# Differential attention on one core: softmax weights of the upper 512 queries taken from the scores of their maxima, turned by 32x32 transposes and DMA

## The chip, the core and the metric

The kernel runs on one core of a Trainium2 chip. The core has five engines that each work through their own instructions in order: TensorE (PE, matmuls; PEld is its weight load), VectorE (DVE), ScalarE (ACT), GpSimd (POOL) and SyncE (SP), which here issues the DMAs. SBUF is the on-chip memory of 128 partitions, PSUM the eight banks of 128 x 512 fp32 into which matmuls write. The metric is the device time of one execution in microseconds (us).

## The reference

Four residual layers over x, two sequences of 1024 tokens of width 512: a gated linear recurrence, a feed-forward with ternary weights, a differential attention, and the same feed-forward again. The change lies in the attention:

```python
q = concat([split(x @ Wq1), split(x @ Wq2)])      # 2 x 16 heads of 32
k2, v2 = repeat(split(x @ Wk), 2), repeat(split(x @ Wv), 2)
scores = where(causal, q @ k2.T / sqrt(32), min)
p = softmax(scores)                                # 1024 x 1024 per head
y1, y2 = halves(p @ v2)
x = x + (y1 - sigmoid(x @ Wlam) * y2) @ Wo
```

Each of the two sequences has 32 query heads. All is fp32, and the scores are large enough that a softmax needs its row's maximum subtracted.

## The kernel before

The stages run one after another: recurrence, first feed-forward (`feed_forward(0, ...)`), attention, second feed-forward. The residual x lives in SBUF all the time, as 16 tiles `xres` of 128 tokens.

The attention goes through 32 pairs: `b` (sequence), `g` (group of projections), `p` and `par`. A pair holds two heads, told apart by `e` (0 or 1). `project` makes queries and keys of a group (three kinds, two halves of the sequence each: six projections for four pairs), and copies each half to the other 64 partitions by DMA (`gr<-gr`), so that a pair's heads can stand in any of four 32-row strips of the PE array: strip `2 * i + e`, where `i` picks the copy (`operands`). A matmul with 32 rows occupies one strip, and four in different strips can run together.

Every score is computed twice. `maxima_bank` (tile `s`, line 947) computes scores with queries on the partitions; DVE takes each row's maximum (lines 958 and 963; on a diagonal block with a causal mask added). `split_maxima` (POOL) splits a maximum into three bf16 parts, `turn_maxima` transposes them on PE (`mt`, line 994), so that they lie along a row. `row_phase` then computes the scores again with keys on the partitions (tile `t`, line 1024), since the product with the values needs keys there, and subtracts the maxima by a bf16 matmul of ones with `mt` (line 1034). ACT takes exp (`pr<-t`, line 1056), POOL zeroes what lies above the diagonal (line 1064) and adds two blocks of keys for the totals (line 1088). `weigh` multiplies with the values and with ones (`y`, line 1109): four 32-column strips, for two halves of the queries and two heads. The result is copied (`ys`) and sent by DMA to `share` (products) and `tot` (totals).

A pair has six steps; in each, PE does scores of this pair, maxima scores of the next, `weigh` of the step before and what `beside` holds (`at(n, step, ...)`): projections of the next group, the next sequence's normalisation, the last sequence's output. PE's order is the written one (`manual_schedule`); DVE and ACT are ordered by the planner until the end of the attention. PSUM: a ring of seven banks and one `edge` bank.

At the end of a sequence `divide` inverts the totals and folds in lambda, `combine` multiplies the factors in and subtracts the two halves, `project_out` multiplies by Wo and adds to `xres`.

## Time and profile before

The median of three runs is 2051.46 us (2048.37 to 2052.23). The profiled execution took 2050.75 us; its span, from first to last instruction, is 2049.0 us.

| stage (us from the span's start) | length | PE busy | DVE busy | ACT busy | POOL busy |
|---|---|---|---|---|---|
| recurrence 0 to 371.8 | 371.8 | 361.2 | 279.9 | 153.8 | 103.6 |
| feed-forward 371.8 to 733 | 361.2 | 361.0 | 153.5 | 144.1 | 77.8 |
| attention 733 to 1684.4 | 951.4 | 942.2 | 531.4 | 382.6 | 526.0 |
| feed-forward 1684.4 to 2049 | 364.6 | 358.0 | 136.3 | 137.7 | 77.3 |

A group's line in the profile gives line, engine, operation, output and inputs by name, shapes and count; then busy us and the mean ns of one instruction; then the idle time before them and what ended it. A timeline line gives start, length, engine and line, with idle time in brackets. A stretch's line gives for each engine its busy time and, in brackets, its instructions, then PE's granted clock (1.00 is full), the share of time that the 16 DMA engines were busy, and GB/s. An fp32 matmul stands as two records in the trace.

### The profile page before, as it was taken

Reading aid. Unit: us, or ns where it says so; the run is one execution under the profiler, and the core shown is the slowest. Engines: PE = TensorE matmul, PEld = TensorE weight load, DVE = VectorE, ACT = ScalarE, POOL = GpSimd, SP = SyncE. Lnnn points to the kernel's source line nnn. Section 1 sums busy time; section 2 is a strip of 40 time slices with the busy share of each in tenths; the row PEclk is TensorE's granted clock in tenths of the full one; section 3 lists DMA queues with packets and bytes.
Section 4 is the critical chain, followed back from the end, with each engine's and each line's share of the span. In section 5 each row is a group of like instructions: output and inputs, shape, how many; then the busy total and the mean of one; then the engine's idle time right before and its main releaser. Section 6 shows DMA issues by size and latency. Waiting matters only on the chain.

```text
span 2049.0 us, 34958 instructions
## 1 busy us (share of the span) xinstructions
PE 2022.5 (99%) x13824; PEld 1290.9 (63%) x13832; DVE 1101.0 (54%) x2375; ACT 818.2 (40%) x1453; POOL 784.6 (38%) x1131
## 2 busy tenths in 40 slices
PE   8999999999999999999999999999999999999998
PEld 4444444788888854555555545565556648888887
DVE  5876868444344434555565556455556554343422
ACT  4444343234333422444444423254444513343433
POOL 1412323122222222666666635365657732222222
PEclk9999999999999999999999999999999999999999
DMA  7121212500000111111111101202110032000000
GB/s 278 65 92 62 88 57 80 222 0 1 1 1 1 37 48 34 48 28 43 28 43 28 43 9 39 60 22 51 25 30 15 15 149 103 21 1 21 0 21 21
DMA packets 77651, 99.14 MB, mean 48 GB/s; under 512 B 41520, under 2 KB 49840, under 8 KB 77488
## 3 DMA queue, kind: packets, MB, share of 16 engines
q1 hardware_dynamic: 77488, 96.92, 14.4%
q8 instruction: 108, 1.77, 0.4%
q14 instruction: 55, 0.45, 0.1%
HBM read 58.75 MB, written 16.78 MB: 37 GB/s over the span
## 4 chain that ended last, share of the span: by engine, by line
PE 92%; DVE 5%; POOL 1%; issue 1%; ACT 1%; DMA 0%; SPq 0%; DVEq 0%; ACTq 0%; POOLq 0%
PE g L664 11%; PE u L664 11%; PE f_out L685 11%; PE y L1109 11%; PE s L947 9%; PE pq L880 8%; PE t L1024 8%; PE pv L842 3%; PE pq L328 3%; PE a_out L546 2%; PE b_out L1187 2%; PE pv L328 2%; PE pa L328 2%; PE pg L328 2%; PE pk L328 2%; PE t L1034 1%
## 5 line engine op out<-in xcount | busy, mean ns | idle before, releaser
L1056 ACT ACTIVATE pr<-t 128x512 f32<-128x512 f32 (+1 forms) x640 | 306.6, 558 | 347.5 <-PE t L1034 294.2
L679 POOL TENSOR_TENSOR ssq<-ssq,sq 128x512 f32<-128x512 f32 x120 | 154.5, 1288 | 589.6 <-ACT sq L678 589.6
L1088 POOL TENSOR_TENSOR pr<-pr,pr 128x384 f32<-128x384 f32 (+1 forms) x256 | 287.1, 1132 | 121.5 <-ACT pr L1056 114.3
L963 DVE TENSOR_REDUCE nmax<-s 128x1 f32<-128x384 f32 (+1 forms) x320 | 183.2, 581 | 201.5 <-PE s L947 200.9
L958 DVE CUSTOM_DVE_ANT_0 s<-s,causal 128x512 f32<-128x512 f32 (+3 forms) x512 | 245.6, 506 | 54.0 <-PE s L947 49.6
L947 PE MATMUL s<-gr,gr 32*128 32x384 f32 (+3 forms) x1664 | 264.0, 480 | 1.9 <-DVE nmax L963 1.9
L670 DVE TENSOR_TENSOR h<-h,u 128x512 f32<-128x512 f32 x128 | 88.1, 688 | 317.5 <-PE u L664 305.4
L664 PE MATMUL g<-xs,w 128*128 128x512 f32 x1024 | 257.7, 394 | 0.0
L685 PE MATMUL f_out<-w,hs 128*128 128x512 f32 x1024 | 254.3, 390 | 0.3 <-DVE hs L673 0.3
L664 PE MATMUL u<-xs,w 128*128 128x512 f32 x1024 | 253.2, 389 | 0.0
L1024 PE MATMUL t<-gr,gr 32*128 32x512 f32 (+3 forms) x1536 | 224.3, 528 | 1.3 <-DVE nmax L963 1.3
L664 PEld LDWEIGHTS u<-xs,w 128*128 128x128 f32 x1024 | 192.2, 188 | 40.6
L685 PEld LDWEIGHTS f_out<-w,hs 128*128 128x128 f32 x1024 | 191.5, 188 | 40.7 <-DVE hs L673 1.1
L664 PEld LDWEIGHTS g<-xs,w 128*128 128x128 f32 x1024 | 190.0, 188 | 39.6 <-issue 1.0
L947 PEld LDWEIGHTS s<-gr,gr 32*128 32x128 f32 x1664 | 172.5, 186 | 45.5 <-issue 15.3
L1109 PE MATMUL y<-pr,val 128*32 128x256 f32 (+3 forms) x3072 | 188.1, 334 | 2.5 <-POOL pr L1088 1.9
L880 PE MATMUL pq<-b_xt,w_qk 128*128 128x512 f32 x384 | 176.0, 603 | 0.8 <-DVE nmax L958 0.8
L1064 POOL TENSOR_SCALAR_AFFINE_SELECT pr<-pr 128x256 f32<-128x256 f32 x256 | 101.9, 410 | 194.5 <-ACT pr L1056 190.9
L672 ACT CAST hs<-h 128x512 fp32r<-128x512 f32 x128 | 79.4, 620 | 234.7 <-DVE h L670 234.7
L669 ACT ACTIVATE h<-g 128x512 f32<-128x512 f32 x128 | 76.6, 599 | 230.5 <-PE g L664 230.4
L1109 PEld LDWEIGHTS y<-pr,val 128*32 128x32 f32 x3072 | 80.3, 109 | 89.4 <-issue 49.7
L673 DVE TENSOR_TENSOR hs<-h,hs 128x512 fp32r<-128x512 f32 x128 | 88.6, 692 | 87.2 <-ACT hs L672 87.2
(169 smaller groups left out, 2555.0 us busy)
## 6 DMA issues: line engine op xcount, KB each, us to landing
w<-w_kept SPq DMA_DIRECT2D x32, 768.0 KB
w_kept<-w SPq DMA_DIRECT2D x16, 768.0 KB
gr<-gr SPq DMA_DIRECT2D x96, 128.0 KB
w<-in_w_gu_dram SPq DMA_DIRECT2D x32, 256.0 KB
share<-ys SPq DMA_DIRECT2D x128, 64.0 KB
x<-in_x_dram SPq DMA_DIRECT2D x16, 256.0 KB
w<-in_w_pt_dram SPq DMA_DIRECT2D x16, 256.0 KB
w_qk<-in_wq_dram SPq DMA_DIRECT2D x8, 512.0 KB
```

The costliest lines, as they stand in the source:

```text
L328: nc.tensor.matmul(po, w[:, k, ts(c, P)], xt[:, k, :], start=(k == 0), stop=(k == NKC - 1))
L664: nc.tensor.matmul(po, ws[f][:, part, ts(k, P)], xs[:, e, k, :], start=(k == 0 and e == 0), stop=(k == NKC - 1 and e == 1),)
L679: nc.gpsimd.tensor_add(ssq, ssq, sq)
L685: nc.tensor.matmul(po[j], hp[:, e, ts(j, P)], ws[f][:, 2, :], start=(f == 0 and e == 0), stop=(f == NF - 1 and e == 1),)
L880: nc.tensor.matmul(po, w[:, k, ts(kind, P)], xts[b][:, k, ts(e, BLK)], start=(k == 0), stop=(k == NKC - 1),)
L947: nc.tensor.matmul(part, queries[:, ts(j, P)], keys[:, first * P : (first + nk) * P], start=True, stop=True,)
L958: nc.vector.tensor_tensor_reduce(part, part, causal[:, BLK - part.shape[-1] :], -1.0, 3.0e38, ALU.add, ALU.min, top,)
L963: nc.vector.tensor_reduce(top, part, AX.X, ALU.max, negate=True)
L1024: nc.tensor.matmul(banks[i, e][:, at_col : at_col + nq], keys[:, ts(kb, P)], queries[:, (qb + 1) * BLK - nq : (qb + 1) * BLK], start=True, ...
L1056: nc.scalar.activation(room[i][:, e, :width], banks[i, e][:, :width], AF.Exp)
L1088: nc.gpsimd.tensor_add(both[:, e], both[:, e], second[:, e])
L1109: nc.tensor.matmul(into[rows, lo // 2 :].rearrange("p (a r) -> p a r", r=64), head, moving[:, e, :].rearrange("p (a h r) -> p a h r", h=2, ...
```

## The change

The lower four query blocks of 128 (j = 0 to 3) of each pair keep the two passes, with smaller parts: the mask is now added on PE by four small bf16 matmuls (`hide`: `select`, whose 32 rows pick 32 positions, times `hidden`), the totals are products with ones of each block of keys, and POOL adds nothing.

The upper four blocks (j = 4 to 7) have one pass. `row_scores` computes a block's scores with queries on the partitions, up to 1024 keys in a PSUM tile of two banks, one tile per head (`ps_rows`, two buffers). `row_maxima` takes the negative maximum on DVE, `row_weights` takes exp on ACT with the maximum as bias and sums the row on the way (`accum_out` into `sums`); it writes the weights in an order that puts every fourth key together. `row_turn` transposes 32x32 squares on DVE into `flat`, and four DMAs carry the squares to `full`, where keys lie on the partitions. `row_outputs`, two slots later, multiplies with the values in pieces of 64 columns. No maxima are split or turned for these blocks, and their totals come from `sums` by one transpose on PE at the end of a sequence (`turn_high`).

A pair now has four slots, one upper block in each, in the order j = 7, 5, 6, 4. The order of PE, DVE and ACT is the written one throughout. The ring of PSUM banks has three banks instead of seven. Copies of the values and of `mt` go from DVE to ACT. To make room, the residual tiles 4 to 15 are written to DRAM (`x_kept`) in the first feed-forward and read back where they are used: eight before the second sequence's normalisation (`fetched`), four for the first sequence's output, and all twelve at the end of the attention.

The core of the diff (the pools, names and the removed functions are left out):

```diff
+        def hide(i, e, part):
+            rows = ts(2 * i + e, HD)
+            for a in range(QB):
+                nc.tensor.matmul(
+                    part[:, a * HD :], select[rows, a, :], hidden[rows, a, a * HD :],
+                    start=False, stop=(a == QB - 1),
+                )
...
+        def low_scores(pair, e, i, js):
+            keys, queries = operands(pair, i, e)
+            po = ring_bank(f"s{name(pair)}_{e}_{js[0]}")
+            at_col, parts = 0, []
+            for j in js:
+                part = po[:, at_col : at_col + (j + 1) * P]
                 nc.tensor.matmul(
+                    part, queries[:, ts(j, P)], keys[:, : (j + 1) * P], start=True, stop=False
+                )
+                hide(i, e, part[:, j * P :])
...
-            nc.vector.tensor_copy(mt, po)
+            nc.scalar.copy(mt, po)
...
+        ROWS = (7, 5, 6, 4)
+        def row_scores(n, step):
+            pair, j = pairs[n], ROWS[step]
+            banks = [ps_rows.tile([P, 2 * BLK], F32, tag="rows", ...) for e in range(2)]
+            for i in range(2):
+                for e in range(2):
+                    keys, queries = operands(pair, i, e)
+                    cols = slice(i * BLK, BLK if i == 0 else (j + 1) * P)
+                    nc.tensor.matmul(
+                        banks[e][:, cols], queries[:, ts(j, P)], keys[:, cols],
+                        start=True, stop=(i == 0),
+                    )
+            for e in range(2):
+                hide(1, e, banks[e][:, j * P : (j + 1) * P])
+            return banks
...
+            nc.scalar.activation(          # row_weights
+                weights[:, :width].rearrange("p (B b k) -> p B k b", b=QB, k=HD),
+                banks[e][:, :width].rearrange("p (B k b) -> p B k b", b=QB, k=HD),
+                AF.Exp, bias=tops[:, e : e + 1],
+                accum_out=sums[b][:, j - QB, at_row : at_row + 1],
+            )
...
+            nc.vector.transpose(           # row_turn
+                flat[n][:, : 2 * width].rearrange("p (b e B q) -> p b e B q", b=QB, e=2, q=HD)[:, :, e],
+                weights[:, :width].rearrange("p (B b k) -> p b B k", b=QB, k=HD),
+            )
+            if e == 0:
+                return
+            full = spread[n, step] = row_room("full", n, step)
+            part = 2 * width // QB
+            for a in range(QB):
+                nc.sync.dma_start(
+                    out=full[:, ts(a, part)],
+                    in_=flat[n][ts(a, HD), : 2 * width].rearrange("k (b r) -> k b r", b=QB),
+                )
...
+            for B in range(j + 1):         # row_outputs
+                for half in range(2):
+                    for e in range(2):
+                        nc.tensor.matmul(
+                            y[ts(2 * half + e, HD)].rearrange("p (a q) -> p a q", q=HD),
+                            val[:, B, ts(4 * g + 2 * p + e, HD)],
+                            full[:, ts(half, 2), e, B, :],
+                            start=(B == 0), stop=(B == j), skip_group_check=True,
+                        )
+            nc.scalar.copy(outs[n][:, ts(j - QB, 2 * HD)], y)
...
+        def fetched(b, j):
+            i = b * NQ + j
+            xn = norm.tile([P, D], F32, tag="xn", name=f"xn_b{i}")
+            nc.sync.dma_start(out=xn, in_=x_kept[i - TPB])
+            xns[b, j] = normal(i, j, stats[b], f"b{i}", xn, xn)
...
+                slot = 2 * i + 3           # projections of the next group
+                at(n + slot // STEPS, slot % STEPS, part(nb, ng, kind, e))
...
+        def slot(n, step):
+            if step == 0 and after:
+                lows = [low_scores(after, e, 0, (0, 2)) for e in range(2)]
+                lows.append(low_scores(after, 1, 1, (1,)))
+            elif step in (1, 2) and pair:
+                lows.append(low_units(pair, step - 1, after and (after, 2 - step, step - 1, (3,))))
+            elif step == 3 and pair:
+                lows.append(high_units(pair, after and (after, 0, 1, (1,))))
+            for one in lows:
+                if one:
+                    low_maxima(*one)
+            if pair:
+                banks = row_scores(n, step)
+                tops = row_maxima(n, step, banks)
+                weights = [row_weights(n, step, 0, banks, tops)]
+            back = STEPS * n + step - 2
+            if 0 <= back < STEPS * PAIRS:
+                row_outputs(*divmod(back, STEPS))
...
+            if pair:
+                weights.append(row_weights(n, step, 1, banks, tops))
+                row_turn(n, step, 0, weights[0])
+            if step == 0 and pair:
+                turn_maxima(pair)
+            if step == 0 and n:
+                share_later(n, step, low_share_out, *low_outputs(pairs[n - 1]))
+            for f in beside.get((n, step), ()):
+                f()
+            if pair:
+                row_turn(n, step, 1, weights[1])
```

`low_units` and `high_units` hold the second pass of the lower blocks (scores with keys on the partitions, subtraction, exp, `cut` on POOL), `low_outputs` their products with values and ones, and `share_later` the DMAs of the results.

## The prediction

> **What bounds the kernel now.** I read the page's busy shares first, then the groups by shape, then TensorE (PE) in order of time through one head pair, then the stretches.

> ```profile
> PE 2022.5 (99%) x13824; PEld 1290.9 (63%) x13832; DVE 1101.0 (54%) x2375; ACT 818.2 (40%) x1453; POOL 784.6 (38%) x1131
> ...
> 898.10 0.39 PE L994 MATMUL mt<-ident,maxima 128*128 128x128 bf16 x4
> 898.41 0.70 PE L947 MATMUL s<-gr,gr 32*128 32x384 f32 x2
> ...
> 901.53 1.14 PE L1024 MATMUL t<-gr,gr 32*128 32x512 f32 x8
> 902.49 0.40 PE L1034 MATMUL t<-mt_s,ones 3*128 3x512 bf16 x4
> 902.71 0.92 PE L947 MATMUL s<-gr,gr 32*128 32x384 f32 x8
> 903.56 0.54 PE L1109 MATMUL y<-pr,val 128*32 128x64 f32 x16
> 903.91 0.40 PE L1109 MATMUL y<-pr,summed 128*32 128x128 f32 x8
> ```

> PE is the bound: each group starts as the one before ends. Four 512-column score matmuls, one in each 32-row strip, take 0.96 us together (901.53 to 902.49): 0.85 of stream, 0.1 of lead-in. So 512 columns of one strip cost 0.85, and four strips run side by side. Bf16 is four times faster (902.49 to 902.71). Four bf16 transposes, each with its own weights, take 0.31 us with lead-in. The 64- and 128-column products (903.56 to 903.91) take 0.35 us together; four of 64 columns are 0.11.

> ```profile
> 894.63:994.05 99.42, 99.42 (x1154) 58.10 (x1153) 56.03 (x185) 45.70 (x96) 61.82 (x113) 1.00 0.15 36
> 910.90:911.90 1.00, 1.00 (x20) 0.46 (x16) 0.77 (x3) 0.42 (x1) 1.00 (x2) 1.00 0.92 209
> 1197.00:1203.00 6.00, 6.00 (x44) 3.25 (x44) 3.22 (x12) 0.87 (x2) 2.58 (x8) 0.50 0.00 0
> 1548.10:1554.90 6.80, 6.73 (x56) 4.25 (x60) 3.85 (x13) 1.18 (x3) 4.15 (x8) 0.50 0.09 20
> ...
> 1190.47 1.17 PE L947 MATMUL s<-gr,gr 32*128 32x512 f32 x4 [1.62 <-DVE nmax L963]
> 1195.78 0.70 PE L1024 MATMUL t<-gr,gr 32*128 32x256 f32 x4 [1.32 <-DVE nmax L963]
> ```

> Four pairs with six projections take 99.4 us, PE never idle. A projection is 3.63 in the chain, so a pair without them is (99.4-21.8)/4 = 19.4. The last two columns of a stretch are DMA share and GB/s: copies inside SBUF reach 209 GB/s. The column before them is PE's granted clock: where PE waited 1.62 and 1.32 us, it stood at 0.50 afterwards, and once more at 1548.

> ```profile
> L963 DVE TENSOR_REDUCE nmax<-s 128x1 f32<-128x384 f32 x256 | 141.9, 554 | 147.3 <-PE s L947 146.7
> L963 DVE TENSOR_REDUCE nmax<-s 128x1 f32<-128x512 f32 x64 | 43.9, 686 | 54.3 <-PE s L947 54.2
> L492 DVE TENSOR_SCALAR prefix<-prefix 128x512 f32<-128x512 f32 x16 | 6.8, 427 | 0.6
> L848 DVE COPY val<-pv 128x512 f32<-128x512 f32 x8 | 5.5, 691 | 14.6 <-PE pv L842 14.6
> L490 DVE TENSOR_TENSOR_SCAN prefix<-a,a_start 128x512 f32<-128x512 f32 x16 | 19.6, 1225 | 0.6
> L958 DVE DVE_READ_ACCUMULATOR2_ANT nmax<- 128x1 f32 x512 | 72.4, 141 | 0.0
> ...
> L1056 ACT ACTIVATE pr<-t 128x512 f32<-128x512 f32 x384 | 202.3, 605 | 105.6 <-PE t L1034 105.6
> L473 ACT ACTIVATE a<-pa,two 128x512 f32<-128x512 f32 x16 | 11.0, 688 | 37.2 <-PE pa L328 37.2
> L478 ACT ACTIVATE gate<-pg 128x512 f32<-128x512 f32 x16 | 9.6, 598 | 44.0 <-PE pg L328 41.3 <-issue 2.7
> ```

> These are the prices of what the change adds: a reduction 0.686 at 512 columns and 1.03 ns per further column; exp 0.605; a bias from a tile 0.09 (688 against 598).

> **The change, part by part.**

> *PE work.* Removed per pair: 3328 of 4608 columns of transposed scores per parity, the subtraction on them, the upper totals, one of two maxima transposes. Added: the causal mask as 64 small bf16 matmuls (four per block and parity: 0.22 us at the pace of the transposes), second totals in the lower half, upper products in 64-column pieces. I add each strip's columns and take the longest strip.
> Slot 0: lower scores 1.5 (512 columns 0.85, two mask sets 0.44, leads 0.2), row scores 0.85, upper products 0.9, transposes 0.35, lower products (2 x 1.07 + lead) 2.3: 5.95. Slot 1: 0.95 + 0.21 + 0.85 + mode lead, products 0.7: 2.8. Slot 2: 2.1 + 1.05 = 3.15. Slot 3: 1.85 + 0.85 = 2.7. Sum 14.6. The same method on the old pair's six steps gives 3.2 + 2.3 + 3.3 + 3.3 + 3.2 + 2.3, and 0.8 for transposes: 18.4 where 19.4 is measured, so 15.4: 4.0 less per pair, 129 us over 32. A mask set is bounded by its columns alone (320, 0.13) and by 0.22 for each matmul (0.88); the transposes, with weights of their own, are nearest. This holds if the mask chains run beside the other strips; one strip after another the pair would be 19.0 and nothing is saved.

> *The ring through the engines.* Row scores of a slot go into two double banks, all of which the second exp of the previous slot frees. So between two row scores lie two reductions in a row and one exp: for 1024 columns 1.21 + 1.21 + exp. The exp is 0.605 + 0.47 + 0.09 + a read of the sum, which I put at DVE's 0.14: 1.30. Its strided store has no row: from no extra to double (2.3); I take no extra, since it still writes each element once. A transpose has no row either: between 0.427 and 1.225 per 512 columns (L492, L490); I take the copy's 0.691, the plain one-input row, so 1.22 for 1024 columns. DVE is then 8.1 + 8.1 + 3.9 = 20.1 us a pair.
> [...]

> A pair with projections in slots 1 and 3, from its slot 0: row scores ready 2.4; DVE, behind five lower reductions, ends the two row reductions at 4.3 and 5.4; exps end 5.7 and 7.2 with a copy between; only then ACT copies the turned maxima (7.8). PE reaches slot 1 at 5.95, where the bank of the lower score and the subtraction wait for that copy: 1.85 idle, rows ready 9.9. Projection until 14.2; its copy (0.6) holds a bank of the ring of three: 0.6 idle, rows ready 16.9. Two reductions and the exp free the banks at 20.75, PE was ready at 19.0: 1.75 idle. Products, projection: 26.1. With 5% on PE's own work, partly inside these waits, 26.4, against 26.7 now (19.4 + 7.26).
> A pair without the projection in slot 1 loses its cover: the second exp, then transposes still queued on DVE ahead of the next reductions, give 24.2 against 23.0. One without that in slot 3 leaves DVE 1.9 late: 24.2 against 23.0. With none, 22.5 against 19.4. A group: 1.2 - 0.3 - 0.3 + 1.2 = +1.8; seven of them +13, the last +12: **+25**. So the 129 us saved go into waits.

> *Squares by DMA.* 1.05, 0.79, 0.92 and 0.66 MB a pair's slots, 3.4 MB. At 209 GB/s 5.0 us for the largest, four issues of 0.6 on SP in front; 16.3 of some 25 us a pair, plus today's 0.15. Products come almost two slots later, so this is hidden by the slots' other work while they take 6 us each; uncovered, the largest costs 1 us a pair. Nothing (a quarter's rows read at full rate) to half the rate (each copy reads 32 partitions; +7 us a pair) are the ends; I take hidden.

> *Residual in DRAM.* Eight tiles come back before their normalisation, behind up to 0.8 MB of squares on the same queue (3.8 us) and SP's issues; PE's transposes of them stand before the next slot's scores. Four slots x 4 us = **+16**. Four more before the output sums, DVE waiting: **+6**. Ends: 0 if landed early, 40. The twelve stores before lie in the feed-forward, where DMA does next to nothing, and the twelve loads at the end have b_out's 28 us over them: nothing; uncovered, 3 MB at 209 GB/s are 15 us.

> *End.* The last pair's lower totals now come last: copy, DMA (about 2.4), a 3.34 us reciprocal (L1156), three small DVE steps, with PE empty: **+8**, ends 3 and 15. POOL loses its adds of pr, and ACT takes the copies of values and turned maxima (0.6 each) from DVE: the first is off the path, the second is in the walk. SP issues 25 DMAs a pair instead of 15 (0.6 each, 15 us of 26): nothing, while a transfer waits for no issue of a later slot.

> *Clock.* 0.50 after the waits above lasted 6.8 us (1548.10 to 1554.90), 3.4 lost, twice in the attention stage, which has thirteen PE waits of 0.25 us or more. Some 96 such waits (three a pair) now: 15 falls by that ratio, 50 us; part lies inside waits: **+35**, ends 0 and 110.
> [...]

> Sum: 25 + 16 + 6 + 8 + 35 = +90 on the profiled execution's own 2050.75 (span 2049.0 and 1.75 around it): 2141, where the median of the three is 2051.46. I predict **2140**.

> **The rivals.**
> 1. *Faster.* The waits close up because exp and reduction overlap better than by their full durations (512-column DVE work in a row starts every 0.6, not 0.69), and PE stays the bound: -129 + 30 for residual and end, 1952. It decides from a loop (reductions plus exp) shorter than PE's slot by about 1 us. For it: PE's work does fall, DVE at 54% has room. Against: slot 2 has no projection, and there reductions plus exp exceed PE's work by 1.75.
> 2. *Transposes at the scan's price.* 2.3 us for 1024 columns: DVE 27 us a pair plus waits: 5 us a pair more, 2300. Against it: a one-input operation.
> 3. *DMA the bound.* At half of 209 GB/s a pair's squares take 33 us where its slots take 25: about +220, 2290. For it: each copy reads 32 partitions. Against: four follow one another.
> 4. *Nothing saved on PE*, the mask chains one after another: 3.6 us more in each pair, most of it on top: 2200. Against: in today's trace a strip's second matmuls start after another strip's first.

> **How the numbers follow.** Forecast 0.46 (of which 0.03 within 0.2%; its own range 2060 to 2210), faster 0.27, transposes 0.12, DMA 0.08, serial masks 0.07. Slower by over 0.2%: 0.43 + 0.12 + 0.08 + 0.07 = 0.70; within 0.2%, about what a measurement can tell from no change: 0.03; faster 0.27. The range 1950 to 2300 goes from the first rival to the second and third.

> **What would show it.** Right: PE busy well under 99% in the attention stage, its idle time before lower scores released by ACT's copy of the maxima and before row scores by exp; clock 0.50 in several stretches; about 26 us a pair in mid-stage. Wrong: PE still without gaps and a pair near 20 (rival 1); DVE busy throughout (2); products waiting for DMA (3); no falls of the clock; transposes far from 1.2 us.

## The result, and the profile after

The changed kernel takes 2353.2 us (median of four, 2347.3 to 2358.7), the kernel before 2049.9 beside it: ratio 1.148, interval 1.145 to 1.151. The forecast said slower, but 2140 with 2300 as the upper end.

The stages before the attention take what they took (733.7 us up to it, 733.9 before). The attention grew from 950.4 to 1253.8 us. Its line among the stretches, the line of one steady group of four pairs with six projections, and one stretch in the middle of that group (length; busy time and instructions of PE, weight load, DVE, ACT, POOL; then PE's granted clock, DMA share, GB/s):

```profile
733.70:1987.50 1253.80, 1160.33 (x13994) 659.31 (x13994) 693.36 (x874) 606.56 (x986) 137.82 (x455) 0.81 0.54 123
955.45:1090.83 135.38, 127.52 (x1697) 72.39 (x1697) 78.25 (x96) 71.10 (x117) 12.98 (x51) 0.80 0.58 127
1021.30:1028.10 6.80, 6.80 (x67) 3.31 (x66) 4.12 (x7) 4.12 (x9) 2.15 (x9) 0.50 0.64 118
```

The same stage before:

```profile
733.90:1684.30 950.40, 941.19 (x9619) 529.20 (x9619) 531.35 (x1596) 382.59 (x776) 525.10 (x929) 0.99 0.15 39
```

The reader should look at the clock: 0.81 over the stage where it was 0.99. A mean of 0.81 says that some 38% of the stage ran at 0.50; the trace's record of the clock has 56 spells in the stage, 484.7 us in all, where before it had 13.7 us. Below, a spell is a stretch of time at 0.50, and half-clock time is the sum of the spells. I use one account for all kernels below: the stage's length less half of its half-clock time is its length at full clock (an estimate: it takes PE at 0.50 for half as fast, as the projection below was, and would overstate the clock's part if PE waited much inside the spells; the runs with idle matmuls test that).

| | attention | at clock 0.50 | length less half of it |
|---|---|---|---|
| before | 950.4 | 13.7 | 943.6 |
| after | 1253.8 | 484.7 | 1011.5 |

So of +303 us, by this account, 235 are clock and 68 are work and waits. The prediction had 35 and 55.

PE in order of time in that group (start, length, engine and line, idle time in brackets):

```profile
1003.58 0.29 PE L1089 MATMUL y<-pr,summed 128*32 128x64 f32 x8
1003.80 1.12 PE L1005 MATMUL t<-gr,gr 32*128 32x512 f32 x4
1006.12 1.12 PE L951 MATMUL s<-gr,gr 32*128 32x512 f32 x2 [1.20 <-ACT mt_s L989]
...
1018.98 0.23 PE L1013 MATMUL t<-mt_s,ones 3*128 3x128 bf16 x2
1020.34 0.69 PE L951 MATMUL s<-gr,gr 32*128 32x256 f32 x2 [1.13 <-ACT yr L1212]
...
1025.50 4.97 PE L908 MATMUL pq<-b_xt,w_qk 128*128 128x512 f32 x8
```

The first idle time is one that the prediction foresaw: a lower score waits for the copy of the turned maxima. In the second, another waits for a bank that ACT's copy of the upper products frees, where the prediction had the projection's copy. Both copies stand behind an exp. After the second the clock is at 0.50 from 1021.3 to 1028.1, and the projection, which has nothing to do with the change and takes 3.70 us in the same view of the kernel before, takes 4.97: 2.60 us in the spell and 2.37 behind it; half of the first and all of the second make 3.67. By that half the spell of 6.8 us costs 3.4 us, the wait itself 1.1.

The groups, split by shape (count; busy us and mean ns of one; idle time before it), and the waits (us, times, longest):

```profile
L1158 ACT ACTIVATE w<-sr,tops 128x1024 f32<-128x1024 f32 x64 | 130.8, 2073 | 184.0 <-DVE tops L1144 184.0
L1158 ACT ACTIVATION_READ_ACCUMULATOR w<-sr,tops 128x1 f32 x256 | 52.9, 207 | 0.0
L1179 DVE STREAM_TRANSPOSE flat<-w 128x1024 f32<-128x1024 f32 x64 | 79.7, 1245 | 56.3 <-ACT w L1158 54.1 <-ACT yr L1212 2.2
L1144 DVE TENSOR_REDUCE tops<-sr 128x1 f32<-128x1024 f32 x64 | 75.4, 1219 | 27.7 <-PE sr L936 27.7
```

```profile
PE s L951 <- ACT yr L1212: 26.0, 23, 1.1
PE s L951 <- ACT mt_s L989: 23.6, 22, 1.2
PE yr L1204 <- DMA full<-flat: 13.9, 11, 4.1
PE r L1247 <- DVE factors L1240: 8.3, 2, 7.7
...
PE sr L1132 <- ACT w L1158: 2.5, 2, 1.5
```

Reduction (1.22) and transpose (1.25) cost what was forecast (1.21, 1.22). Exp with its sum takes 2.07 + 0.21, where 1.30 was taken. The products' waits for the squares are 14 us in all, and the end's wait for the factors is the forecast 8. The wait that the prediction gave 1.75 us in a pair, of upper scores for the exp that frees their banks, comes twice in the whole stage (2.5 us).

### The profile page after: what moved, and what is told of

It is laid out like the page before. It is cut to its first block, busy times and chain, and to the rows that moved or that the text cites. A ratio compares the mean times of both kernels' runs of the same rounds, so it can differ in the third digit from the quotient of the medians.

```text
span 2352.2 us, 43504 instructions
## 1 busy us (share of the span) xinstructions
PE 2241.3 (95%) x18184; PEld 1420.0 (60%) x18192; DVE 1262.5 (54%) x1652; ACT 1040.6 (44%) x1661; POOL 394.9 (17%) x653
## 4 chain that ended last, share of the span: by engine, by line
PE 76%; DVE 6%; ACT 5%; SPq 4%; DMA 4%; issue 3%; POOL 0%; ACTq 0%; DVEq 0%; POOLq 0%
PE g L673 10%; PE u L673 10%; PE f_out L694 10%; PE pq L908 7%; PE s L951 7%; PE sr L1132 5%; ACT w L1158 5%; PE yr L1204 4%; DMA full<-flat 4%; DVE tops L1144 3%; PE b_out L1264 2%; PE pv L873 2%; PE pq L337 2%; SPq L1188 2%; PE a_out L555 2%
## 5 line engine op out<-in xcount | busy, mean ns | idle before, releaser
L1158 ACT ACTIVATE w<-sr,tops 128x1024 f32<-128x1024 f32 (+3 forms) x256 | 432.6, 1712 | 343.3 <-DVE tops L1144 343.2
L1179 DVE STREAM_TRANSPOSE flat<-w 128x1024 f32<-128x1024 f32 (+3 forms) x256 | 267.3, 1044 | 188.1 <-ACT w L1158 184.9
L1144 DVE TENSOR_REDUCE tops<-sr 128x1 f32<-128x1024 f32 (+3 forms) x256 | 250.1, 1018 | 88.7 <-PE sr L936 88.7
L951 PE MATMUL s<-gr,gr 32*128 32x512 f32 (+3 forms) x512 | 232.2, 561 | 49.7 <-ACT yr L1212 26.0
L1132 PE MATMUL sr<-gr,gr 32*128 32x512 f32 (+3 forms) x1024 | 242.2, 722 | 3.0 <-ACT w L1158 2.5
L963 DVE TENSOR_REDUCE nmax<-s 128x1 f32<-128x128 f32 (+3 forms) x256 | 116.4, 482 | 212.4 <-PE s L936 110.2
L936 PEld LDWEIGHTS <-select 32*128 32x128 bf16 x2048 | 142.9, 111 | 135.9 <-issue 110.2
L1204 PE MATMUL yr<-full,val 128*32 128x64 f32 x6656 | 168.8, 270 | 13.9 <-DMA full<-flat 13.9
L1204 PEld LDWEIGHTS yr<-full,val 128*32 128x32 f32 x6656 | 141.3, 142 | 67.4 <-issue 49.9
L951 PEld LDWEIGHTS s<-gr,gr 32*128 32x128 f32 x512 | 89.1, 216 | 111.9 <-ACT mt_s L989 43.9
```

Of the source, the lines that this page charges most:

```text
L936: nc.tensor.matmul(part[:, a * HD :], select[rows, a, :], hidden[rows, a, a * HD :], start=False, stop=(a == QB - 1),)
L951: nc.tensor.matmul(part, queries[:, ts(j, P)], keys[:, : (j + 1) * P], start=True, stop=False)
L963: nc.vector.tensor_reduce(nmax[pair][:, j, e : e + 1], part, AX.X, ALU.max, negate=True)
L1132: nc.tensor.matmul(banks[e][:, cols], queries[:, ts(j, P)], keys[:, cols], start=True, stop=(i == 0),)
L1144: nc.vector.tensor_reduce(tops[:, e : e + 1], banks[e][:, : (j + 1) * P], AX.X, ALU.max, negate=True)
L1158: nc.scalar.activation(weights[:, :width].rearrange("p (B b k) -> p B k b", b=QB, k=HD), banks[e][:, :width].rearrange("p (B k b) -> p B k ...
```

## The experiments

Each time is a median of four or five runs beside seven of the kernel before. My theory after the result was A: the exp's strided store was the failed term, and everything else follows from the longer loop. Against it stood B, that PE's own work did not fall as counted; C, that the clock is the price; and DMA, rival 3.

### Where the stride stands: e1, e5, e13

The store in a row, the stride moved to the transposes' read:

```diff
-                weights[:, :width].rearrange("p (B b k) -> p B k b", b=QB, k=HD),
-                banks[e][:, :width].rearrange("p (B k b) -> p B k b", b=QB, k=HD),
+                weights[:, :width],
+                banks[e][:, :width],
...
-                weights[:, :width].rearrange("p (B b k) -> p b B k", b=QB, k=HD),
+                weights[:, :width].rearrange("p (B k b) -> p b B k", b=QB, k=HD),
```

> The exp writes its 128 x (j+1)*128 weights in a row, as it reads them, and the 32x32 transposes pick every fourth key on their reading side instead. Theory A (the strided store doubles the exp, and the exp is in the loop that frees the score banks): the 1024-column exp falls from 2.07 to 1.1 to 1.3 us, the transposes stay at 1.25, some 4 us a pair go at once (130 us) and with shorter waits some of the 488 us at half clock: 2060 to 2190 us. Theory B (the sum taken along the way or the bias doubles the exp): the exp stays at 2.07, time within 15 of 2353. Theory C (the exp only fills time in which PE is slow because of its clock): the exp falls to 1.2, the time by less than 60.

2325.0 us, ratio 1.134 (1.133 to 1.136). Its two groups:

```profile
L1158 ACT ACTIVATE w<-sr,tops 128x1024 f32<-128x1024 f32 x64 | 71.8, 1121 | 194.7 <-DVE tops L1144 194.7
L1179 DVE STREAM_TRANSPOSE flat<-w 128x1024 f32<-128x1024 f32 x64 | 129.5, 2060 | 7.7 <-ACT w L1158 7.7
```

Exp falls from 2073 to 1121 ns, so the store's stride was its extra, neither bias nor sum; the transpose rises from 1245 to 2060. The price went with the stride, here from ACT's store (as written, each element 128 bytes from the one before) to DVE's read (16 bytes). The time falls by 28 us only: inside what C asked (less than 60), far from A's 2060 to 2190.

Then the stride goes to PE: the upper scores read the keys with every fourth together, and the added mask is laid out to match.

```diff
-                        banks[e][:, cols], queries[:, ts(j, P)], keys[:, cols],
+                        banks[e][:, cols].rearrange("p (B b k) -> p B b k", b=QB, k=HD),
+                        queries[:, ts(j, P)],
+                        keys[:, cols].rearrange("p (B k b) -> p B b k", b=QB, k=HD),
```

> Both layouts plain: the matmuls of the upper scores read the keys with every fourth together, so that scores already lie in the squares' order; exp reads and writes in a row, the transposes read in a row, and the added mask is laid out to match. This is the case that the prediction's sum assumed (exp of 1024 columns 1.30 with its sum, transposes 1.22). Theory A (the store was the failed term, the rest of the sum holds): exp about 1.12 plus 0.21, transposes about 1.24, group of four pairs near 101 to 108 us, 2100 to 2180 us, clock above 0.95. Theory B (PE's own work did not fall, or the new mix of small matmuls lowers the clock by itself): the exp gets shorter just the same, but the time stays above 2230 us with clock below 0.93. Theory C (reading keys with a stride costs PE): matmuls of the upper scores well over 0.72 us each.

2303.1 us, ratio 1.124 (1.122 to 1.126). Theory A falls: it asked for 2100 to 2180. So does the hope that PE reads with a stride at no cost. The upper scores' instructions (minimum, median and maximum ns), changed kernel, then this one:

```profile
L1132 PE MATMUL sr<-gr,gr x1024: 270/601/1218, 765.6 to 1930.1; 32*128 32x512 f32 x92, 32*128 32x256 f32 x30, 32*128 32x384 f32 x29, 32*128 32x128 f32 x20
```

```profile
L1140 PE MATMUL sr<-gr,gr x1024: 400/1072/1244, 762.4 to 1880.4; 32*128 32x512 f32 x96, 32*128 32x256 f32 x32, 32*128 32x384 f32 x22, 32*128 32x128 f32 x21
```

From the first upper score of slot 1 to its first product it is 2.01 us at full clock, where it was 1.08. The stride costs PE's read too; e13, below, keeps this layout of the masks, reads keys in a row and is back at 1.08.

Last, the reordered keys are stored once for a group by ACT (four copies of 64 partitions), so that exp, transposes and scores are all plain:

```diff
+                for i in range(2):        # and the same for the second half of the keys
+                    nc.scalar.copy(
+                        groups[b, g, "turned"][:64, i, :].rearrange("p (B b k) -> p B k b", b=QB, k=HD),
+                        po[ts(i, 64)].rearrange("p (B k b) -> p B k b", b=QB, k=HD),
+                    )
```

> The reordered keys come from a second tile, made by ACT once for a group by four copies of 64 partitions with a strided store; exp, transposes and upper scores are all plain now. This is what the prediction's sum assumed of every duration. Theory A (the store was the one failed term): 2100 to 2160 us. Theory B (PE's own 18.9 us a pair, where 15.4 was counted, is the base): the kernel that read its keys with a stride paid 0.94 us a slot for it, 120 us in all, and without them 2180 is left; 2160 to 2220 us.

2290.8 us, ratio 1.118 (1.114 to 1.121). The durations on ACT and DVE are now near those that the prediction assumed, and 62 us are gone, where down to 2140 it would be 213. Both expectations miss: the 120 us of PE reads taken away gave 12. The attention is 1195.9 us, 406.2 at half clock; the products' waits for DMA rose from 14 to 62 us. What one engine gave up, the next wait took.

### PE's own work: e9, e10, e14

Nearly all of the upper half's work beside PE is left out (the reductions and an exp of 128 columns stay, the products read a constant tile):

```diff
-            width = (j + 1) * P           # exp; the sum (accum_out) left out as well
+            width = P
...
-            nc.vector.transpose(...)      # and the four DMAs of squares
+            spread[n, step] = constant
```

> The changed kernel with nearly all of the upper half's work beside PE left out: exp on 128 columns without its sum, no transposes, no square copies; the upper products read a constant tile. PE's matmuls are all there in their order, so this is PE's own work with the waits of the lower half alone. The prediction's count (15.4 us a pair in place of 19.4): attention some 129 us shorter than before, 1930 to 1990 us in all, clock above 0.97. Mask chains that run one after another (rival 4: 19.0 a pair): 2040 to 2080 us at full clock. The mix lowering the clock without waits: clock below 0.94 and more than 2100 us with few waits recorded.

2076.6 us, ratio 1.014 (1.010 to 1.018), clock 0.975. PE alone is already slower than the whole kernel before. From the first upper score of a slot to that of the next, at full clock, the four slots take 5.97, 3.94, 3.73 and 5.23 us: 18.9 a pair (18.4 where two slots also hold a projection, its 3.63 taken off), where 15.4 was counted and 19.4 is the old pair. It is rival 4's 19.0. Slot 0's lower scores show why (PE in order of time, this kernel):

```profile
1035.44 0.48 PE L951 MATMUL s<-gr,gr 32*128 32x128 f32 x2
1035.77 0.30 PE L936 MATMUL s<-hidden,select 32*128 32x128 bf16 x4
1035.92 0.89 PE L951 MATMUL s<-gr,gr 32*128 32x384 f32 x2
...
1036.87 0.27 PE L951 MATMUL s<-gr,gr 32*128 32x128 f32 x1
1036.98 0.30 PE L936 MATMUL s<-hidden,select 32*128 32x128 bf16 x4
1037.13 0.89 PE L951 MATMUL s<-gr,gr 32*128 32x384 f32 x2
...
1038.41 0.71 PE L1132 MATMUL sr<-gr,gr 32*128 32x512 f32 x3
```

The second head's scores (another strip) start at 1036.9, after the first head's whole chain: 2.97 us up to the upper scores, where 1.5 was counted. The reading to be tested is that a matmul that waits for its own strip holds up those for other strips written behind it. So the next kernel changes that order alone:

```diff
-                lows = [low_scores(after, e, 0, (0, 2)) for e in range(2)]
-                lows.append(low_scores(after, 1, 1, (1,)))
+                lows = low_scores_mixed((after, 0, 0, (0, 2)), (after, 1, 0, (0, 2)), (after, 1, 1, (1,)))
...                                        # one score of each strip, then one mask of each; and in row_scores
-            for e in range(2):
-                hide(1, e, ...)
+            for a in range(QB):
+                for e in range(2):
+                    nc.tensor.matmul(part[:, a * HD :], select[rows, a, :], hidden[rows, a, a * HD :], ...)
```

> PE's matmuls alone as in the kernel with the upper half's other work left out, and its omissions; only the order on PE is changed: the lower scores of slot 0 and the masks of the two heads take turns between the strips, instead of one strip's scores and masks before the next strip's. Theory 'order' (a chain in one strip holds up the strips behind it, since PE starts its matmuls in order): the 2.97 us of slot 0's lower scores fall towards the 1.5 that the prediction counted and the mask sets of the upper scores halve, 2 to 2.5 us a pair, 2000 to 2020 us. Theory 'count' (each of the 64 added matmuls has its price wherever it stands): within 15 us of 2077.

2019.1 us, ratio 0.986 (0.984 to 0.988): 58 us less by the medians (e9's executions lie between 2067 and 2089), 42 us between the two profiled executions. The time is what the theory of order asked; the work, below, is not. The stretch of slot 0 now:

```profile
1052.06 1.24 PE L972 MATMUL s<-gr,gr 32*128 32x384 f32 x5
1052.83 0.30 PE L979 MATMUL s<-hidden,select 32*128 32x128 bf16 x6
...
1053.68 0.29 PE L979 MATMUL s<-hidden,select 32*128 32x128 bf16 x6
1053.79 0.70 PE L1158 MATMUL sr<-gr,gr 32*128 32x512 f32 x2
```

1.73 us instead of 2.97. But a whole pair, from slot to slot as above, falls only from 18.9 to 18.3 us (18.4 to 17.7 with projections taken off), where 2 to 2.5 were expected: slot 1, for one, now takes 2.75 us to its first product where e9 took 2.16, because its lower score starts behind the second pass's scores and no longer beside them (why, is not shown). And not all of the gain is work: by the account the stage falls from 918.8 to 895.1 at full clock (24 us), and half-clock time from 102.4 to 61.4 (20 us). Before the change of order, slots 0 without anything beside them had a mean of 1.63 us at half clock although PE's waits were as few (9 idle times of 0.25 us or more, 10 here); with it they have none. Of e9's 19 spells 15 (75 us) have no idle time of 0.25 us or more in the 7 us before them, and 10 of these begin 0.5 to 0.8 us after the first upper score of slot 0, right behind the chains. So here the clock fell without a wait, and the order of the matmuls decided it. Why it fell, no run here shows.

In the changed kernel itself the same edit has ACT and DVE around it:

> The changed kernel with one thing changed: the order on PE, so that the strips take turns in the lower scores of slot 0 and in the masks of the upper scores. In PE's work alone this was worth 58 us. If one strip's chains bring the clock down by themselves, half-clock time falls from 485 us below 350 and the time to 2230 to 2290. If the waits for ACT and DVE bring it down, PE only waits longer: 2310 to 2350, half-clock time as before.

2305.0 us, ratio 1.124 (1.122 to 1.126): 48 us less, half-clock time 484.7 to 409.6. Between the two expectations: 75 us of half-clock time go with the chains, the larger part stays, and so do its waits (29 us for the turned maxima, 26 for the products' copy).

### The clock: e2, e15, e17

Six idle matmuls ahead of each slot's upper products, into unused columns of their bank:

```diff
+            for _ in range(6):
+                nc.tensor.matmul(whole[:, P:], ones, idle, start=True, stop=True)
```

> The changed kernel with six idle bf16 matmuls of 384 columns (0.16 us each, 123 us in all over 128 slots) ahead of each slot's upper products, into unused columns of their bank; nothing reads them. Theory A (half clock has a price of its own, brought on by PE's pauses): the 488 us at clock 0.5 shrink to under half, and the time falls to 2200 to 2320 in spite of the added work. Theory C' (the clock falls only while PE waits anyway, and costs nothing): the time stays or grows, 2353 to 2470.

2320.4 us, ratio 1.132 (1.130 to 1.134): more work on PE, and 33 us faster (20 between the profiled executions). At an estimated 0.163 us each (in the trace of before a bf16 matmul of 512 columns is followed by the next after 0.216 to 0.22 us, three quarters of which are 0.162 to 0.165) the 768 matmuls are 125 us; the stage's length at full clock rose by 104 and half-clock time fell from 484.7 to 242.3. Later, four in each slot of the kernel of e12 (below):

> The kernel with copied keys, strips in turn and the products' copy on DVE, with four idle bf16 matmuls of 128x128 by 384 columns ahead of the upper products of each slot, some 82 us of added PE work at full clock. If the clock sets the price: half-clock time below 230 us and the time within 30 us of 2230, perhaps below it. If the clock's account is only a label on waits: 2270 to 2310 us.

2225.6 us, ratio 1.085 (1.084 to 1.087), against 2230.3. The two stages, without and with:

```profile
733.50:1867.40 1133.90, 1003.91 (x13994) 597.61 (x13994) 693.82 (x1002) 463.49 (x882) 138.79 (x457) 0.84 0.58 135
```

```profile
731.00:1855.20 1124.20, 1023.68 (x14506) 577.36 (x14506) 693.54 (x1002) 465.01 (x882) 139.13 (x458) 0.93 0.58 136
```

By the same estimate 83 us of matmuls were added (512 x 0.163), and the length at full clock rose by just that (958.1 to 1040.6), while half-clock time fell from 351.6 to 167.3, worth 92. PE's idle time fell by 30 us only (130 to 101), so if the clock cost nothing the stage should have grown by some 54 us; it shrank by 10. The account is no label: half-clock time can be sold for work.

Whether it happens with the old work too, once PE waits, is asked of the kernel before, with one size changed:

```diff
-            tc.tile_pool(name="b_ring", bufs=7, space=bass.MemoryType.PSUM, reuse_waits="tile")
+            tc.tile_pool(name="b_ring", bufs=4, space=bass.MemoryType.PSUM, reuse_waits="tile")
```

> The kernel before, with one size changed: its ring of PSUM banks has four instead of seven, so that PE waits for banks, with the old work and order. If waits of about a microsecond bring the clock down, half-clock time rises from 14 us to more than 100 and the time to 2120 to 2300, more than the recorded waits alone add. If it is the new work: half-clock time stays below 50 us, and the time rises by no more than the waits.

2504.5 us, ratio 1.221 (1.218 to 1.224). Stage and largest wait of PE:

```profile
736.80:2135.20 1398.40, 1312.31 (x9619) 660.02 (x9619) 551.61 (x1596) 389.28 (x776) 527.91 (x929) 0.88 0.10 27
```

```profile
PE s L947 <- ACT pr L1056: 76.9, 124, 1.8
```

Half-clock time rises from 13.7 to 331.1 us with the old work; the recorded waits are 0.6 us on average. The time overshot the expectation: of 448 us more in the stage 289 are length at full clock, and only 86 are recorded as PE's idle time. Four banks cost more here than the idle column shows; what the rest is was not tried, so this run does not show that waits alone do it. E16, below, comes closer.

### Order of ACT and PE: e3, e4, e7, e11, e12

The upper products ahead of the upper scores, and the maxima turned ahead of the first exp, so that neither copy stands behind an exp (with the strided store, and with e1's store):

```diff
             back = STEPS * n + step - 2
             ...
                 row_outputs(*divmod(back, STEPS))
+            if pair:
+                banks = row_scores(n, step)
+                if step == 0:
+                    turn_maxima(pair)
+                tops = row_maxima(n, step, banks)
```

> The changed kernel, with upper products written ahead of the row scores of their slot, and the turned maxima and their copy ahead of the first exp; the exp still stores with a stride. If PE's waits for the copies of maxima and products (some 50 us on PE) are a loss of their own, 2230 to 2310; if the exp alone sets the pace, 2340 to 2360.

> Store in a row and the other order together. If PE's own work fell by about 129 us, as the prediction had it, and waits and clock were all that stood against it: 1950 to 2080 us, DVE the busiest of the other engines. If PE's work did not fall (mask chains one after another): not under 2080.

2534.5 us (1.236, 1.235 to 1.238) and 2478.8 us (1.209, 1.208 to 1.211): both far slower than the changed kernel, and the first outside both of its expectations. The products' bank is one of the ring of three, and in this place they stand right behind the lower scores and units that hold the ring; PE's waits there, of the first of the two, are for the readers of those:

```profile
PE yr L1204 <- ACT pr L1050: 109.1, 28, 4.0
PE yr L1204 <- DVE nmax L963: 100.5, 54, 3.3
```

They were 0 in the changed kernel, where the upper scores stand between and give the readers time. Half-clock time is 655 us in the first, 170 more than in the changed kernel.

Moving only the turned maxima, on top of e5:

> The kernel with both layouts plain, and the maxima of the lower blocks turned right behind the upper scores of slot 0, so that ACT copies them while it would wait for the first upper maximum. Theory A: the waits of lower scores for that copy (23.6 us in the changed kernel) and the falls of the clock behind them go: 30 to 60 us less than the kernel without this move. Theory B: within 20 us of it, since falls come from the mix. The rival that ends on the other side: the transposes of the maxima now stand ahead of the upper products and wait for POOL or for a bank: 10 to 40 us more.

2299.4 us (1.123, 1.117 to 1.127), against 2303.1: no difference that can be told. The expectation took its 23.6 us from the changed kernel; in e5, whose exp is shorter, the waits for this copy were down to 0.4 us already, so there was nothing to move. The falls of the clock stayed (369 us of half clock in e5, 406 here).

The two below are e13's kernel with the turned maxima early and the strips in turn, and that with the products' copy on DVE:

> As the kernel with copied keys, and the strips take turns in PE's order and the maxima of the lower blocks are turned right behind the upper scores. Theory B: PE's own work falls by 2 to 2.5 us a pair, but only where PE sets the pace; 40 to 90 us less than with copied keys alone. Theory A: PE's order matters little since its time goes into waits: within 30 us.

> As the one before, and the copy of the upper products goes from ACT, where it stands behind an exp, to DVE, where it stands behind the second upper maximum. If the waits of lower scores for this copy (13.3 us in 26 places with the strided keys) also bring the clock down behind them: 20 to 60 us less. If they are covered by the next wait of the loop: within 10 us. On the other side: DVE waits for the products ahead of its transposes: 10 to 30 us more.

2232.7 us (1.090, 1.087 to 1.093) and 2230.3 us (1.089, 1.087 to 1.090). The first gives 58 us against e13, within its expectation for B (two changes at once; the early maxima alone gave nothing that can be told in e7). The second gives nothing that can be told.

### DMA: e8, e16

The squares are read where the transposes put them:

```diff
-            full = spread[n, step] = row_room("full", n, step)
-            ...                            # four DMAs
+            spread[n, step] = flat[n]
```

> The changed kernel with the square copies left out: the upper products read the transposed tile directly, so their values are not the reference's; exp keeps its strided store. Hidden, as the prediction had it: only the waits of products and residual tiles for DMA go (13.9 us and some 10 to 20), and the time is 2310 to 2355. DMA as the bound (rival 3): 2250 or less, some 100 us or more gone.

2335.2 us, ratio 1.139 (1.138 to 1.141): 18 us. In the changed kernel the copies are hidden. The same edit on e12:

> The kernel with copied keys, strips in turn and the products' copy on DVE (2230 us), with the square copies left out, so that the upper products read the transposed tile directly and their values are not the reference's. Its waits of products for DMA are 65 us. If these also bring the clock down: 2100 to 2170 us and half-clock time below 250 us (it was 352). If the clock falls for other reasons: 2180 to 2225.

2107.3 us, ratio 1.027 (1.025 to 1.030): 123 us. Its stage at full clock falls by 30 only (958.1 to 928.5); half-clock time falls from 351.6 to 143.4, worth 104. PE has the same matmuls in the same order in both; what goes is e12's largest wait, which in e16 is not there:

```profile
PE yr L1262 <- DMA full<-flat: 64.8, 47, 3.9
```

With these waits, 65 us, some 208 us of half-clock time go. One of them in PE's order of time, and the stretch that follows:

```profile
1043.78 0.31 PE L1262 MATMUL yr<-full,val 128*32 128x64 f32 x4 [0.53 <-DMA full<-flat]
1046.05 1.92 PE L1262 MATMUL yr<-full,val 128*32 128x64 f32 x60 [1.96 <-DMA full<-flat]
```

```profile
1046.00:1057.00 11.00, 10.73 (x146) 7.17 (x147) 6.07 (x9) 3.26 (x8) 2.11 (x9) 0.50 0.82 168
```

PE stands for two microseconds in slot 2, while the DMA engines are busy (share 0.82 just after), and then works for eleven at half clock. Hidden work is hidden behind something: once exp, transposes and order were cheap, PE waited for the copies.

No kernel with the whole computation comes below 2225 us, and PE's matmuls alone, in the better of the two orders tried, take 2019: with everything else hidden, that order would win some 30 us against the kernel before.

## Why the prediction was wrong

**Clock: the step that failed most.** It forecast 15 falls and +35 us, ends 0 and 110. Shown: 56 falls in the stage of 8.7 us on average (6.8 was taken), 485 us at 0.50, 235 of the 303 us. That waits bring falls was right: 50 of the 56 spells have an idle time of 0.25 us or more in the 7 us before them, while only 40% of the stage's moments have one. The count of waits was not the fault (PE has 67 idle times of 0.25 us or more in the attention where 96 were forecast). The ratio was: two falls to thirteen waits were taken from a kernel where only three of these waits are over 1 us (1.62, 1.32 and 1.15), and seven come between 1630 and 1653 us without a fall; in the changed kernel 55 of 67 are over 1 us, with chains written strip by strip between (slot 0's lower scores, 2.97 us from 1030.39 to 1033.36). The length of a wait does not settle it alone, since e15's falls follow waits of 0.6 us on average; what does was not tried. E16 shows half-clock time going with the waits, e15 shows the clock falling with the old work once PE waits for banks, e9 and e10 show falls that come from the order of the matmuls without waits; e2 and e17 show that the lost time is real.

**PE work: wrong by 3 us a pair.** "This holds if the mask chains run beside the other strips" was the condition, and it did not hold: 18.4 to 18.9 us a pair in e9, rival 4's 19.0, where 15.4 was taken. By the account PE's matmuls alone need 25 us less than the whole stage before, not 129. The reason given against rival 4, that a strip's second matmuls start after another strip's first, was read from matmuls written in turn; the change writes its chains strip by strip. E10 shows the lower scores of slot 0 at 1.73 us once they take turns, near the counted 1.5, but the pair still at 17.7 to 18.3. At full clock the scores of the four slots, up to the first product, take 4.3, 2.2, 2.9 and 3.0 us in e9 and 2.9, 2.75, 2.9 and 3.0 in e10, where 2.35, 2.0, 2.1 and 1.85 were counted; products and transposes take what was counted. So half of the miss stands in slot 0, and the order of its chains is shown as the cause of most of that half. What the half in slots 2 and 3 is made of, masks in chains or the count itself, was not tried.

**Exp: the store was mis-sized.** No extra was taken, because each element is still written once; it measured 2.07 + 0.21, at the upper end that was named (2.3). E1 shows the stride as its cause. Alone it was worth less than its 0.95 us an instruction suggests: 62 us at most over three kernels, since PE, DVE and DMA stand close behind it.

**The sum without the clock was near (55 forecast, 68 measured), for the wrong reason.** Forecast were 129 us less of work and 184 more of waits. Measured are 25 us less of work (e9) and 84 more of PE's idle time in the stage (9 to 93). Two terms missed by some 100 us each and nearly cancel: that is luck. The wait of upper scores for exp is all but absent (2.5 us): the likely reason, not tried alone, is that PE, with the work that it kept, came to them later.

**What held.** The direction; the wait of lower scores for the turned maxima; reduction and transpose (rival 2 falls at 1.25 us); the end (+8, measured 7.7); the residual tiles (+16 forecast, 12.6 us of PE's idle time before their transposes; what this cost beyond was not tried); copies hidden in this kernel (18 us, so rival 3 falls here). Their price once uncovered was put at 32 us and measured 123 in e12, since the wait takes the clock with it (104 of the 123).

Rival 1, the faster one, needed PE to stay the bound with 129 us less work: e9, with 25, takes its ground away.

## What to carry to other kernels

Price a strided fp32 access like these at what was measured here, 1.85 times one in a row on ACT, 1.65 on DVE and 1.86 on PE (slot 1's upper scores), and place it where it is done once. Count matmuls of different strips as side by side only if they stand in turn in PE's order (here slot 0's lower scores took 1.73 us in turn, 2.97 strip by strip). When a change puts waits of about a microsecond every few microseconds into a PE that was always busy, price the clock from a kernel that waits that often, or take what was measured here, 235 us of clock beside 93 us of idle time; a hidden step's price is found only after what hides it is made cheap.
